# A cross-attention kernel in fp32: a new order for all operations, and two of the last half stores on ScalarE's queue

## The chip, the cores and the metric

The kernel runs on one core of one Trainium2 chip. The metric is the time of one execution in device microseconds (us). Before the change the median of three runs is 582.59 us. One execution was also profiled: every instruction with its engine, its start and its duration.

## The reference, cut to what matters

```python
query = hidden_states @ Wq                       # x: (2, 2048, 640)
keyt, valt = enc @ Wk, enc @ Wv                  # enc: the first 124 rows of ctx (2, 128, 384)
hs = _mha(query, keyt, valt)                     # 8 heads, softmax over 124 keys
ca_q1 = einsum('btc,th->bch', ca, Wq_ca)         # ca: the last 4 rows of ctx
ca_q1 = ca_q1[:, indices, :]                     # 384 rows stretched to 2048 by a fixed index
ca_hs1 = _mha(ca_q1, residual, residual)         # attention over the 2048 rows of x
ca_hs2 = _mha(ca_hs1 @ Wq, ca @ Wk_ca, ca @ Wv_ca)
out = (hs + ca_hs2) @ Wout + b_out + residual    # (2, 2048, 640), fp32
```

Because `ca_q1` has only 384 different rows, the second branch is computed once for 384 rows per batch and then gathered to 2048 by the index.

## The kernel before

**Units.** The 4096 rows of x are cut into 16 units of 256 rows, two tiles of 128 each. For each unit the kernel computes the text branch: scores of the queries against the 124 keys (`sc`), exponentials and row sums (`p`, `r`, in `softmax`, L2150), a multiply of `p` by the reciprocal sums (`share` in the same function, which POOL, VectorE or ScalarE may do; on ScalarE it is eight pieces, one for each head), a transpose to `eb`, and a store of `eb` to a buffer `kept` in HBM. Later the unit's probabilities come back in another layout in one load of 1 MB, `pT<-kept` (`probabilities`, L2214). There are two buffers for `pT`; a unit's load must wait until the unit that had the buffer has finished its last product `ph`.

**The output product.** `text_out_fast` (L2364) makes `ph` = values times `pT` in three products (`ph_m_0`, `ph_m_2`, `ph_m_4` for unit m; the last frees the `pT` buffer), copies them to `hs`, forms four sums s1 to s4 of halves of `hs` (`hs<-hs`, on VectorE or POOL), and multiplies them with `Wout` and sums of parts of `Wout` in four chains (`po_m_0` to `po_m_3`, a scheme after Strassen that saves one product in eight). After each step of a chain VectorE adds `po` into the unit's rows.

**The rows.** The rows hold x at first: `residual` (L2302) loads each tile of x into one of eight row buffers, four in the tile `x_more` and four in `last_rows`. When the additions to a tile are done, POOL adds the second branch by an indirect DMA (`add_second`, L2321, called "the gather" below), and a store sends the tile out (`stored`, L2479), which frees the row buffer for the next load. The last unit, 15, is different: its gathers come right after its loads, and it leaves in four half stores of 128x320, each as soon as its additions are done (`stored_half`, L2471).

**Other stages.** Around this run the loads and weights at the start, the queries of eight blocks of 512 rows, and the second branch (`s`, `ea`, `acc`, `y`, `away` and `landing` are names of it). Steps of all stages are interleaved on TensorE.

**What sets the order.** No loop order and no scheduler of the compiler: a recorder, `Desk` (L62), collects the operations of all stages as tasks. The table `TURNS` (L83) gives each operation of each task a number. `run` takes the operations in the order of these numbers; the number modulo 6 is the engine:

```python
ENGINES = ("PE", "ACT", "DVE", "POOL", "SP", "NONE")
op = min((op for q in self.queue.values() for op in q), key=turn)
engine = self.ENGINES[turn(op) % len(self.ENGINES)]
```

Each engine then executes its instructions strictly in that order. All loads and stores go out on SP's queue (`dma`, L443), so a load that must wait for a store to land, or a store that must wait for a gather, holds up every transfer behind it. The gathers go out on POOL, between POOL's own arithmetic. `Desk` also has a model of durations (`transfer`, L448, and the figures given to `dma`). The model only decides which free buffer an operation takes; the chip does not see it.

**How its lines read in the profile.** An instruction carries the line of the helper that issued it: L394 a product, L403 a product in four column groups of 32 (`by_columns`), L408 a transpose, L425 any instruction of VectorE, ScalarE or POOL, L445 a DMA on SP, L2323 a gather. So tiles, not lines, tell the steps apart. In the changed kernel these lines stand one further down.

Of the kernel before, what the change touches and what calls it, by code (L numbers as in the profile page):

```python
# [14 lines left out]
P = 128  # L15
# [50 lines left out]
class Desk:  # L66
# [376 lines left out]
    def dma(self, out, in_, us, issue=0.38, more=2.0):  # L443

        self.pin(self.nc.sync.dma_start(out, in_))  # L445
        self.transfer("SP", us, issue, more)
# [11 lines left out]
def kernel(  # L458
# [1343 lines left out]
    def y_rows(b, sb):  # L1802
# [3 lines left out]
        for u in range(2):  # L1806
# [11 lines left out]
            def away(t=op.value, u=u):  # L1818
                dma(kept[:, :, u, :], t.rearrange("p (a n) -> p a n", a=4), 0.8, 0.53)
# [743 lines left out]
```

## Time and profile before

| | us |
|---|---|
| median of 3 runs | 582.59 (581.97 to 584.22) |
| the profiled execution | 581.76 |
| its span, from the first to the last instruction | 579.8 |
| TensorE busy in it | 566.5 (98%) |
| VectorE busy | 390.7 (67%) |
| ScalarE busy | 290.9 (50%) |
| POOL busy | 160.3 (28%) |

PE is TensorE, DVE VectorE, ACT ScalarE, POOL GpSimd, SP the engine that issues the DMAs, and SPq its queue. A row of a timeline has the start in us, the duration, the engine, the line, the operation, out<-in and the shapes; x16 says that 16 like instructions were put together; square brackets hold the idle time of the engine ahead of the row and what ended it. A row of the waits has what the engine waited for, the sum in us, how often, and the longest. A row of the DMA issues has the size of one transfer in KB and the median us from issue to landing. The span is 1.96 us shorter than the profiled execution's time, which includes what lies around it.

### The profile page before, as it was taken

Reading aid. Unit: us, or ns where it says so; the run is one execution under the profiler, and the core shown is the slowest. Engines: PE = TensorE matmul, PEld = TensorE weight load, DVE = VectorE, ACT = ScalarE, POOL = GpSimd, SP = SyncE. Lnnn points to the kernel's source line nnn. Section 1 sums busy time; section 2 is a strip of 40 time slices with the busy share of each in tenths; the row PEclk is TensorE's granted clock in tenths of the full one; section 3 lists DMA queues with packets and bytes.
Section 4 is the critical chain, followed back from the end, with each engine's and each line's share of the span. In section 5 each row is a group of like instructions: output and inputs, shape, how many; then the busy total and the mean of one; then the engine's idle time right before and its main releaser. Section 6 shows DMA issues by size and latency. Waiting matters only on the chain.

```text
span 579.8 us, 18971 instructions
## 1 busy us (share of the span) xinstructions
PE 566.5 (98%) x8115; PEld 308.3 (53%) x8115; DVE 390.7 (67%) x663; ACT 290.9 (50%) x813; POOL 160.3 (28%) x213
## 2 busy tenths in 40 slices
PE   8999999999999999999999999999999999999996
PEld 8885334555555455565554554554554445455442
DVE  3356999999999656557999989996333225433352
ACT  1222264467665699899847762445554663101000
POOL 9102023411310127012025042423404032054171
PEclk9999999999999999999999999999999999999999
DMA  8998486756848796445464987978178457598987
GB/s 238 210 226 137 143 178 177 144 158 140 226 148 154 217 229 167 160 152 179 139 217 152 335 232 263 240 254 247 37 227 219 140 125 250 158 250 270 259 150 226
DMA packets 145213, 112.69 MB, mean 194 GB/s; under 512 B 82405, under 2 KB 116581, under 8 KB 145130
## 3 DMA queue, kind: packets, MB, share of 16 engines
q1 hardware_dynamic: 139498, 100.80, 60.1%
q0 software_dynamic: 5632, 10.69, 10.8%
q8 instruction: 64, 1.05, 0.8%
q14 instruction: 19, 0.16, 0.1%
HBM read 71.23 MB, written 40.22 MB: 192 GB/s over the span
## 4 chain that ended last, share of the span: by engine, by line
PE 75%; DMA 7%; DVE 7%; SPq 4%; ACT 2%; issue 2%; POOL 2%; DVEq 0%; ACTq 0%; POOLq 0%
PE po L403 23%; PE pq L403 19%; PE acc L394 7%; PE sc L394 6%; PE ph L394 6%; PE s L394 6%; PE pq L394 3%; SPq L445 3%; DVE mx L425 2%; DMA last_rows<-in_x_dram 2%; PE pyz L394 2%; DMA last_rows<-o,query 2%; DVE xt L425 1%; DMA xi<-in_x_dram 1%; ACT ea L425 1%
## 5 line engine op out<-in xcount | busy, mean ns | idle before, releaser
L425 DVE TENSOR_REDUCE mx<-s 128x4 f32<-128x2048 f32 x48 | 109.1, 2273 | 2.4 <-PE s L394 2.0
L425 ACT ACTIVATE p<-sc,m 128x124 f32<-128x124 f32 x256 | 90.4, 379 | 40.0 <-DVE m L425 40.0
L425 ACT ACTIVATE ea<-s 128x2048 f32<-128x2048 f32 x48 | 90.6, 1888 | 32.6 <-PE s L394 32.6
L425 POOL TENSOR_TENSOR p<-p,r 128x992 f32<-128x992 f32 x20 | 38.9, 1943 | 169.7 <-DVE r L425 148.8
L403 PE MATMUL po<-wout_sums,hs 128*32 128x320 f32 x1024 | 78.7, 433 | 1.4 <-POOL hs L425 1.4
L403 PE MATMUL po<-wout_sb,hs 128*32 128x320 f32 x928 | 72.1, 434 | 1.0 <-POOL hs L425 0.9
L403 PE MATMUL pq<-xt,wq_sb 128*32 128x256 f32 (+1 forms) x928 | 66.3, 418 | 0.0
L425 DVE TENSOR_TENSOR last_rows<-last_rows,po 128x320 f32<-128x320 f32 x64 | 30.3, 482 | 46.9 <-PE po L403 46.7
L425 ACT ACTIVATION_READ_ACCUMULATOR p<-sc,m 128x1 f32 x256 | 56.4, 220 | 0.0
L425 DVE TENSOR_TENSOR x_more<-x_more,po 128x320 f32<-128x320 f32 x64 | 30.5, 482 | 37.6 <-PE po L403 37.3
L394 PE MATMUL acc<-ea,y_sb 128*32 128x384 f32 (+2 forms) x768 | 50.4, 383 | 0.1
L403 PEld LDWEIGHTS po<-wout_sums,hs 128*32 128x32 f32 x1024 | 31.9, 110 | 35.0 <-POOL hs L425 2.7
L394 PE MATMUL ph<-pT,vpad 128*32 128x256 f32 x768 | 48.0, 380 | 1.0 <-DMA pT<-kept 1.0
L425 DVE TENSOR_REDUCE m<-sc 128x4 f32<-128x496 f32 x64 | 40.8, 663 | 11.6 <-PE sc L394 11.2
L425 POOL TENSOR_TENSOR hs<-hs 128x256 f32<-128x256 f32 x29 | 27.2, 1029 | 71.1 <-ACT hs L425 31.2
L403 PEld LDWEIGHTS po<-wout_sb,hs 128*32 128x32 f32 x928 | 29.0, 110 | 32.1 <-POOL hs L425 1.5
L425 DVE STREAM_TRANSPOSE eb<-p 128x1024 f32<-128x1024 f32 x32 | 39.5, 1236 | 5.6 <-POOL ca L425 2.4
L403 PEld LDWEIGHTS pq<-xt,wq_sb 128*32 128x32 f32 x928 | 28.1, 110 | 28.4 <-issue 12.7
L425 ACT COPY hs<-ph 128x512 f32<-128x512 f32 (+1 forms) x24 | 13.6, 573 | 54.2 <-PE ph L394 54.1
L2323 POOL DMA_INDIRECT x_more<-o,query x16 | 25.5, 1593 | 53.0 <-DVE x_more L425 45.5
L394 PEld LDWEIGHTS sc<-kmain,q 64*128 64x128 f32 x512 | 31.4, 187 | 14.5 <-issue 8.3
L394 PE MATMUL sc<-kmain,q 64*128 64x124 f32 x512 | 37.6, 284 | 0.2 <-ACT q L425 0.2
(219 smaller groups left out, 835.1 us busy)
## 6 DMA issues: line engine op xcount, KB each, us to landing
kept<-eb SPq DMA_DIRECT2D x32, 512.0 KB, 4.6
pT<-kept SPq DMA_DIRECT2D x16, 1024.0 KB, 7.6
landing<-away SPq DMA_DIRECT2D x15, 512.0 KB, 4.8
xi<-in_x_dram SPq DMA_DIRECT2D x56, 128.0 KB, 4.3
x_more<-in_x_dram SPq DMA_DIRECT2D x16, 320.0 KB, 5.2
last_rows<-in_x_dram SPq DMA_DIRECT2D x16, 320.0 KB, 4.0
out_dram<-x_more SPq DMA_DIRECT2D x15, 320.0 KB, 4.7
out_dram<-last_rows SPq DMA_DIRECT2D x15, 320.0 KB, 4.1
```

The costliest lines, as they stand in the source:

```text
L394: self.pin(self.nc.tensor.matmul(out, lhsT, rhs, **kw))
L403: self.pin(self.nc.tensor.matmul(out[j : j + 32], lhsT[:, j : j + 32], rhs, **kw))
L425: self.pin(getattr(engine, what)(*args, **kw))
L445: self.pin(self.nc.sync.dma_start(out, in_))
L2323: desk.pin(nc.gpsimd.indirect_dma_start(out=t, out_offset=None, in_=o2_of[b], in_offset=bass.IndirectOffsetOnAxis(ap=query[:, st : st + 1] ...
```

## The change

The diff replaces the whole table `TURNS`, so every engine has a new order and some operations a new engine. Of its rows only the last unit's half stores are shown, since the others tell a reader nothing: `.71` is the task of unit 15, `.71.3.9` to `.71.3.12` are its half stores, and the second number of each is the store's turn. In the new table two of them have remainder 1, which is ScalarE. The rest of the diff lets `dma` issue on ScalarE and gives other figures to the model of durations.

```diff
@@ -83,210 +83,211 @@
-        ".71.3.5": [11642], ".71.3.6": [12626], ".71.3.7": [13041], ".71.3.8": [13709], ".71.3.9": [13667, 13672],
-        ".71.3.10": [13643, 13648], ".71.3.11": [13697, 13702], ".71.3.12": [13721, 13726], ".71.3.13": [13392,
+        ".71.3.8": [13709], ".71.3.9": [13673, 13675], ".71.3.10": [13637, 13642], ".71.3.11": [13697, 13699],
+        ".71.3.12": [13721, 13726], ".71.3.13": [13476, 13556, 13584, 13598, 13608, 13622, 13680, 13712],
...
-        self.flights = {"SP": [0.0] * self.SLOTS, "POOL": [0.0] * self.SLOTS}
+        self.flights = {e: [0.0] * self.SLOTS for e in ("SP", "POOL", "ACT")}
...
     def dma(self, out, in_, us, issue=0.38, more=2.0):
 
-        self.pin(self.nc.sync.dma_start(out, in_))
-        self.transfer("SP", us, issue, more)
+        self.pin((self.nc.scalar if self.engine == "ACT" else self.nc.sync).dma_start(out, in_))
+        self.transfer(self.engine, us, issue, more)
...
-            dma(kept_of[m][:, :, k], eb.rearrange("p j h a -> p j (h a)"), 1.48, 0.53)
+            dma(kept_of[m][:, :, k], eb.rearrange("p j h a -> p j (h a)"), 1.6, 0.55, 1.6)
...
-            "SP", lambda: dma(pT.rearrange("p i k h a -> p i (k h a)"), by_keys, 2.8, 0.38),
+            "SP", lambda: dma(pT.rearrange("p i k h a -> p i (k h a)"), by_keys, 2.85, 0.42, 2.6),
...
-                dma(t, x[b, st * P : (st + 1) * P, :], 0.75, 0.37)
+                dma(t, x[b, st * P : (st + 1) * P, :], 0.95, 0.37)
...
-        desk.transfer("POOL", 1.7, 1.57)
+        desk.transfer("POOL", 2.0, 1.57, 2.2)
...
-        yield Do("SP", lambda: dma(out[b, st * P : (st + 1) * P, cols], t[:, cols], 0.43, 0.37, 1.8))
+        to = out[b, st * P : (st + 1) * P, cols]
+        yield Do(("SP", "ACT"), lambda: dma(to, t[:, cols], 0.43, 0.45, 2.2))
```

Counted over the program: TensorE has the same 4522 matrix instructions with the same shapes. Of the 32 multiplies of `p`, POOL has 11 (20 before), VectorE 8 (3), ScalarE 13 (9). Of the 64 sums `hs<-hs`, POOL has 32 (29) and VectorE 32 (35). Four of the 128x512 copies of `ph` go from ScalarE to VectorE. SP has 358 transfers (360), ScalarE 2 (0).

Three places of the order matter for what follows. The first is SP's order while units 4 and 2 fetch their probabilities. Names are tiles with their unit, `kept_11` being the probabilities of unit 11, `pT_4` those of unit 4 on their way back, `x_more` rows of x; a number at the end only counts tiles. Before (a second load of `x_more`, two rows behind the first, is left out):

```order
L445 DMA pT_4_4208<-kept_4_2134 128x4x512
L445 DMA y_sb_109<-y_1_1_2809 32x4x256
L445 DMA y_sb_109<-y_1_3_3204 32x4x256
L445 DMA away_7_4104<-wq_sums_836 32x4x256
L445 DMA y_sb_109<-y_1_2_2547 32x4x256
L445 DMA away_7_4104<-x_sums_864 32x4x256
L445 DMA kept_11_4185<-eb_11_1_4289 512x1x256
L445 DMA y_sb_109<-y_1_3_3204 32x4x256
L445 DMA x_more_3129<-in_x_dram 128x640
L445 DMA away_7_4104<-x_sums_864 32x4x256
L445 DMA zb_1_2_1_4359<-z_1_2_2548 128x512
L445 DMA pT_2_4344<-kept_2_1635 128x4x512
```

and now:

```order
L446 DMA landing_823<-away_6_3089 128x1x1024
L446 DMA y_sb_109<-y_1_0_2165 32x4x256
L446 DMA x_more_3071<-in_x_dram 128x640
L446 DMA y_sb_109<-y_1_1_2824 32x4x256
L446 DMA kept_11_4137<-eb_11_1_4260 512x1x256
L446 DMA zb_1_2_1_4296<-z_1_2_2564 128x512
L446 DMA pT_4_4245<-kept_4_2133 128x4x512
L446 DMA pT_2_4275<-kept_2_1640 128x4x512
L446 DMA o2_0_3976<-o2_0_2_4238 128x640
```

Unit 4's load has moved behind the store of `kept_11`, and unit 2's follows it at once.

The second place is SP's order when units 3, 12 and 9 fetch theirs, with the stores of finished rows (`out_0_dram`) and the loads of x into the same row buffers. Before:

```order
L445 DMA pT_3_5700<-kept_3_1923 128x4x512
L445 DMA pT_12_5745<-kept_12_4403 128x4x512
L445 DMA out_0_dram<-last_rows_4391 128x640
L445 DMA out_0_dram<-x_more_3129 128x640
L445 DMA last_rows_4391<-in_x_dram 128x640
L445 DMA x_more_3129<-in_x_dram 128x640
```

and now:

```order
L446 DMA x_more_3071<-in_x_dram 128x640
L446 DMA pT_3_5704<-kept_3_1915 128x4x512
L446 DMA out_0_dram<-last_rows_4257 128x640
L446 DMA last_rows_4257<-in_x_dram 128x640
L446 DMA out_0_dram<-x_more_3071 128x640
L446 DMA x_more_3071<-in_x_dram 128x640
L446 DMA pT_12_6017<-kept_12_4427 128x4x512
L446 DMA pT_14_6168<-kept_14_4836 128x4x512
L446 DMA pT_9_5766<-kept_9_3627 128x4x512
```

Unit 12's load no longer follows unit 3's; two stores and two loads of rows stand between, and each load comes right behind a store instead of behind both.

The third place is the end of POOL's order: sums of halves of `hs`, and gathers into `last_rows` and `x_more`. Before (the fourth and fifth rows are the gathers of unit 15, the sixth is the sum s2 of unit 8):

```order
L2323 DMA last_rows<-o_1_6359,query 128x640 x3
L425 TENSOR_TENSOR hs_4127<-hs_4127 128x256
L425 TENSOR_TENSOR hs_4229<-hs_4229 128x256 x2
L2323 DMA last_rows<-o_1_6359,query 128x640
L2323 DMA x_more<-o_1_6359,query 128x640
L425 TENSOR_TENSOR hs_4229<-hs_4229 128x256
L2323 DMA x_more<-o_1_6359,query 128x640 x2
L2323 DMA last_rows<-o_1_6359,query 128x640
L2323 DMA x_more<-o_1_6359,query 128x640
L2323 DMA last_rows<-o_1_6359,query 128x640 x2
```

and now:

```order
L426 TENSOR_TENSOR hs_4155<-hs_4155 128x256
L2324 DMA last_rows<-o_1_6386,query 128x640
L426 TENSOR_TENSOR hs_4247<-hs_4247 128x256
L2324 DMA last_rows<-o_1_6386,query 128x640
L2324 DMA x_more<-o_1_6386,query 128x640 x3
L2324 DMA last_rows<-o_1_6386,query 128x640
L2324 DMA x_more<-o_1_6386,query 128x640
L2324 DMA last_rows<-o_1_6386,query 128x640 x2
L2324 DMA x_more<-o_1_6386,query 128x640
L2324 DMA last_rows<-o_1_6386,query 128x640
```

The sum of unit 8 is gone from POOL (it is VectorE's now), and behind the last sum only gathers follow. Earlier on POOL, not shown, the sums s2 and s4 of unit 2 stand one gather and one multiply of `p` further ahead than before.

More of the change, by code (lines that the diff above doesn't have):

```diff
@@ L1679, in part_away @@
             def part_away(i, k=k, z=z):
-                dma(away[k, :, i].rearrange("q (g n) -> q g n", g=4), z[:, i].bitcast(F32), 0.45, 0.45)
+                dma(away[k, :, i].rearrange("q (g n) -> q g n", g=4), z[:, i].bitcast(F32), 0.31, 0.45)
             op = yield Do("ACT", lambda: desk.a_copy(z[:, 0], pq[:, cols]), [at], rank=0)
@@ L1706, in rest_back @@
         yield Do(
-            "SP", lambda: dma(t.rearrange("p g n -> p (g n)"), by_rows, 1.45, 0.5), [op.at], marks=[("landed", m)],
+            "SP", lambda: dma(t.rearrange("p g n -> p (g n)"), by_rows, 2.0, 0.56), [op.at], marks=[("landed", m)],
             rank=0,
@@ L1818, in away @@
             def away(t=op.value, u=u):
-                dma(kept[:, :, u, :], t.rearrange("p (a n) -> p a n", a=4), 0.8, 0.53)
+                dma(kept[:, :, u, :], t.rearrange("p (a n) -> p a n", a=4), 0.85, 0.53)
             yield Do("SP", away, frees=[(yts, op.slots[0][0])], marks=[("y out", b, sb, u)], rank=0.5)
@@ L2081, in second @@
             yield Do(
-                "SP", lambda: dma(o2_of[b][ct * P : (ct + 1) * P, :], o2, 1.1, 0.37),
+                "SP", lambda: dma(o2_of[b][ct * P : (ct + 1) * P, :], o2, 1.2, 0.37),
                 [("o2 part", b, ct, 0), ("o2 part", b, ct, 1)], frees=[(eas, k)],
```

405 rows, old and new, of the table TURNS are left out of this document.

## The prediction, as it was put on record before the changed kernel ran

> **What bounds the kernel now.** I read the page's busy times first, then the table of waits of TensorE, then the gaps in the timelines of PE, POOL and SP.
>
> ```profile
> PE 566.5 (98%) x8115; PEld 308.3 (53%) x8115; DVE 390.7 (67%) x663; ACT 290.9 (50%) x813; POOL 160.3 (28%) x213
> core 0: 579.8 us, clock 0.998
> PE po L403 <- POOL hs L425: 2.3, 2, 1.4
> PE s L394 <- ACT ea L425: 1.2, 2, 1.0
> PE unread L394 <- DVE zeros L425: 1.1, 1, 1.1
> PE ph L394 <- DMA pT<-kept: 1.0, 1, 1.0
> PE s L394 <- DVE mx L425: 0.6, 1, 0.6
> PE pt_x L408 <- DVE first_rows L425: 0.5, 1, 0.5
> PE sc L394 <- ACT q L425: 0.2, 1, 0.2
> ```
>
> TensorE is busy for 566.5 of 579.8 us at the full clock. The other 13.3 us are these waits (6.9 together), the tail behind the last product (about 5.7, below), and 0.7 of small change. So no order of the same work can take more than some 12 us off, and an order that starves TensorE can lose any amount. The diff leaves TensorE's work alone: the same products, each shape equally often, in another order. What decides is which of the seven waits go, which new ones come, and what the tail does. These are the gaps that the new order can reach:
>
> ```profile
> 333.86 1.07 PE L394 MATMUL ph<-pT,vpad 128*32 128x256 f32 x16 [1.00 <-DMA pT<-kept]
> 349.39 2.90 PE L403 MATMUL po<-wout_sb,hs 128*32 128x320 f32 x40 [0.92 <-POOL hs L425]
> 555.08 1.28 PE L403 MATMUL po<-wout_sums,hs 128*32 128x320 f32 x16 [1.38 <-POOL hs L425]
> ```
>
> The number in brackets is the idle time ahead. The waits for `ea`, `mx`, `q`, `first_rows` and `zeros` belong to steps whose neighbours read the same in both orders; I leave them as they are (3.6 together, 0 in the sum).
>
> **The sums on POOL: −2.30.** POOL ahead of the second and the third gap:
>
> ```profile
> 342.89 1.35 POOL L425 TENSOR_TENSOR hs<-hs 128x256 f32<-128x256 f32 x1
> 344.41 1.57 POOL L2323 DMA_INDIRECT x_more<-o,query  x1 [0.17 <-issue]
> 345.42 2.43 POOL L425 TENSOR_TENSOR p<-p,r 128x992 f32<-128x992 f32 x1
> 347.22 2.12 POOL L425 TENSOR_TENSOR hs<-hs 128x256 f32<-128x256 f32 x2
> ...
> 550.87 1.55 POOL L2323 DMA_INDIRECT last_rows<-o,query  x1 [12.40 <-DMA last_rows<-in_x_dram]
> 552.73 1.55 POOL L2323 DMA_INDIRECT x_more<-o,query  x1 [0.31 <-issue]
> 553.70 1.33 POOL L425 TENSOR_TENSOR hs<-hs 128x256 f32<-128x256 f32 x1
> ```
>
> At 347 the two sums of unit 2 stand behind a gather and a 2.43 us multiply of `p`; they end at 349.34 and the product starts at 349.39. In the new order both stand ahead of that gather, and the multiply is ScalarE's: at least 1.57 + 2.43 = 4.0 us less ahead of a product that was 0.92 late, so this wait goes whole. At 553 the sum of unit 8 stands behind the two gathers of unit 15, which themselves waited 12.40 us for unit 15's rows. In the new order unit 8's sums are all VectorE's, and POOL keeps only gathers behind that point: 1.38 goes. Together 0.92 + 1.38 = 2.30.
>
> The sum goes where 128x256 sums cost less, and the multiply goes to ScalarE as eight pieces:
>
> ```profile
> L425 DVE TENSOR_TENSOR hs<-hs 128x256 f32<-128x256 f32 x35 | 14.8, 432 | 12.7 <-ACT hs L425 7.6 <-POOL hs L425 4.9
> L425 ACT ACTIVATE p<-p,r 128x124 f32<-128x124 f32 x72 | 21.8, 389 | 4.3 <-DVE r L425 4.3
> 540.00:560.00 20.00, 18.62 (x292) 9.03 (x288) 9.09 (x22) 1.17 (x2) 7.92 (x6) 1.00 0.81 204
> ```
>
> Over the program 9 multiplies leave POOL, 5 go to VectorE and 4 (32 pieces, 32 × 0.389 = 12.4 us on the page's rate) to ScalarE; POOL takes 3 more `hs` sums net, and four copies of `ph` go from ScalarE to VectorE. VectorE is busy 9.09 of 20 us around the last sum (columns: length, then busy time and count of PE, PEld, DVE, ACT, POOL, then clock and DMA share), and ScalarE half of the span, so I cost these at nothing. Cover gone, one piece of 0.389 or one sum of 0.432 on the path would be the price.
>
> **Units 4 and 2 load their probabilities side by side: −1.00 + 0.60.**
>
> ```profile
> 314.50 0.57 SPq L445 DMA_DIRECT2D pT<-kept  x1
> 320.01 0.54 SPq L445 DMA_DIRECT2D kept<-eb  x1
> 325.82 0.43 SPq L445 DMA_DIRECT2D pT<-kept  x1
> ...
> 325.85 1.05 PE L394 MATMUL ph<-pT,vpad 128*32 128x256 f32 x16
> ...
> pT<-kept SPq DMA_DIRECT2D x16, 1024.0 KB, 7.6
> ```
>
> Unit 4's load left at 314.50 for a product at 325.85; unit 2's left at 325.82 for one that stood ready at 332.86 and started at 333.86. In the new order both leave one behind the other, behind the store of unit 11's probabilities (the row at 320.01). For unit 2 that is a lead of some 12 us against 7.6 to land: its wait of 1.00 goes. For unit 4 the lead shrinks. If nothing else moved, the load would leave at about 321.0 and have 4.9 us: 2.7 us late. But PE has two steps ahead of the product that stood behind it, a chain step (1.26 in the row at 572.87 below) and a small one of scores (0.5, an estimate): 6.7 us. And of the 5.5 us of issues between 314.50 and 320.01 several no longer stand ahead of the store; with half of them gone it is 9.5 us. So it is 0.9 late or not at all. I take 0.60, with 0 to 2.7 for the range.
>
> **Unit 12's load behind two store-and-load pairs: +0.70.**
>
> ```profile
> 434.73 3.75 SPq L445 DMA_DIRECT2D pT<-kept  x2
> 448.32 0.35 SPq L445 DMA_DIRECT2D out_dram<-last_rows  x1
> 448.78 0.37 SPq L445 DMA_DIRECT2D out_dram<-x_more  x1
> 453.96 0.34 SPq L445 DMA_DIRECT2D last_rows<-in_x_dram  x1
> 454.63 0.34 SPq L445 DMA_DIRECT2D x_more<-in_x_dram  x1
> ...
> 467.48 1.05 PE L394 MATMUL ph<-pT,vpad 128*32 128x256 f32 x16
> ...
> SPq L445 <- DMA out_dram<-last_rows: 25.0, 9, 6.8
> SPq L445 <- DMA out_dram<-x_more: 19.0, 8, 9.6
> ```
>
> Before, unit 12's load is the second of the row at 434.73, 30 us ahead of its first product at 467.48. In the new order it takes the buffer that unit 3's product frees, and stands on SP behind a store, a load into the same rows, a second store and a second load. A load into rows waits until their store has landed: 448.32 to 453.96 is 5.64 us, 448.78 to 454.63 is 5.85. Before, the two stores went out side by side and waited together; in the new order one pair follows the other: 448.32 + 5.64 + 0.34 + 5.85 + 0.34 = 460.5 for unit 12's load, 468.1 with 7.6 to land, 0.6 late; I round up to 0.70, since the first store may leave a little later too. Bounds: 0, if one pair is 0.7 quicker; if one store keeps SP waiting as long as the 9.6 of the last row, 0.7 + 3.75 = 4.5.
>
> **Other new waits: +1.00.** All 16 units' steps change places, and the loads of units 5 and 15 stand nearer to their products. The old table left three waits of about a microsecond at places that a reordering reaches (3.30 in all); nothing in the trace tells how many a new one leaves beyond the two that I found. I put one, at the size of the pT wait, 1.00, with 0 and 3.30 as bounds.
>
> **The tail: −0.40.**
>
> ```profile
> 572.87 1.26 PE L403 MATMUL po<-wout_sb,hs 128*32 128x320 f32 x16
> 573.66 1.03 DVE L425 TENSOR_TENSOR x_more<-x_more,po 128x320 f32<-128x320 f32 x2 [1.13 <-PE po L403]
> 572.30 2.84 SPq L445 DMA_DIRECT2D out_dram<-last_rows  x3
> 575.25 1.05 SPq L445 DMA_DIRECT2D out_dram<-x_more  x2
> 574.00:576.00 2.00, 0.13 (x4) 0.00 (x0) 0.64 (x2) 0.00 (x0) 0.00 (x0) 1.00 0.78 290
> ```
>
> The last product ends at 574.13, the last addition at 574.69; SP is still issuing until 575.14, so the last half store goes out about 1.05 us later than its data allow (575.74 against 574.69), and the span ends at 579.8. With two half stores on ScalarE, idle here, that 1.05 is the most to be had. The least is 0: the DMA engines are 0.78 busy from 574 to 576, with stores that were issued before. How long an issue on ScalarE takes no row here shows; the rows on SP (0.34) and POOL (1.55) bound it. Nearer to the busy DMA: −0.40.
>
> The Trainium skill, page "DMA: Bandwidth & Descriptors", section "Issuing engines are not separate DMA queues", says that transfers started by different engines share the same 16 DMA engines, and that a second issuing engine saves only issue time. By it this term lies between 0 and the 1.05 above; read strictly, with the engines as the limit, it is 0, and the sum would give 581.5. No row here shows a ScalarE store.
>
> **The sum.** −2.30 − 1.00 + 0.60 + 0.70 + 1.00 − 0.40 = −1.40 on the profiled execution: 581.76 becomes 580.36 (span 579.8 becomes 578.4). The median of the three runs is 582.59, 0.83 above the profiled one; the same step from there gives 581.2.
>
> **Rivals.** *The waits go and nothing comes back* (A). For it: three places have a cause that the order removes, and the two priced losses are within a microsecond of none. Against: a table of this size left seven waits before. −3.30 − 1.05 = −4.35: 578.2.
>
> *SP blocks at the head of its queue* (B, slower). The place is unit 12's load. For it: the two rows of SP's waits, 25.0 and 19.0 us in 17 waits, up to 6.8 and 9.6; before, nothing urgent stood behind them, now a load with no slack does. Against: it takes a long wait in one of two given pairs. With both at their longest: (9.6 − 5.85) + (6.8 − 5.64) = 4.9 more, so −1.40 + 4.9 = +3.5: 586.1. It turns slower than before from 1.4 us more waiting on.
>
> *The waits only move* (C). Each wait of before has a successor elsewhere, and the ScalarE stores bring nothing because the DMA engines finish the same transfers in the same time: 0, 582.6. For it: the kernel stands at 98% TensorE in both orders; against it, the named causes do go.
>
> **How the numbers follow.** Forecast 0.52 (581.2, own range 579.6 to 583), A 0.20, B 0.18, C 0.10. What a measurement of this kernel can tell from no change is about 0.5%, 2.9 us: below 579.7 counts as faster, above 585.5 as slower. A lies below 579.7, and some of the forecast: 0.20 + 0.07 = 0.27 faster. B lies above 585.5 in most of its cases, and the forecast with 3.30 and 2.7 at their upper bounds comes near: 0.17 + 0.02 = 0.19 slower. The rest, 0.54, is within. The range 577.8 to 585.4 leaves out the best of A (0.06) and the worse half of B (0.12).
>
> **What would show it.** In the table of TensorE's waits, `po <- POOL hs` gone or under 0.3 us; `ph <- DMA pT<-kept` at 1 to 2 us, at units 4 and 12, and not at unit 2; POOL behind 550 us with gathers alone; the last half stores issued within 0.5 us of the last addition, and the end under 5.7 us behind the last product. The forecast is wrong if a wait of over 2 us appears at `ph` (B), if new waits of TensorE for additions into row buffers or for PSUM banks add up to over 3 us, or if PE's busy time itself moves by over 1 us, as no term here allows for that.

## The result, and the profile after

The changed kernel runs in 578.02 us (median of 20 runs, 576.45 to 580.68); the kernel before, on the same chips, in 581.56 (20 runs, 579.08 to 584.22). The ratio is 0.9942, with a 95% interval of 0.9927 to 0.9957: 3.4 us less (2.5 to 4.2). The profiled execution took 578.33 us, its span is 576.5, against 581.76 and 579.8 before.

The page's busy times, and then the table of TensorE's waits, to be held against those in the prediction:

```profile
PE 566.8 (98%) x8115; PEld 311.3 (54%) x8115; DVE 395.6 (69%) x666; ACT 297.4 (52%) x840; POOL 151.3 (26%) x211
```

```profile
PE po L404 <- DVE x_more L426: 1.5, 2, 1.1
PE s L395 <- ACT ea L426: 1.2, 2, 1.0
PE s L395 <- DVE mx L426: 1.2, 2, 0.8
PE unread L395 <- DVE zeros L426: 1.1, 1, 1.1
PE pt_x L409 <- DMA xz<-in_x_dram: 0.2, 1, 0.2
PE acc L395 <- ACT ea L426: 0.2, 1, 0.2
```

The work is the same (566.8 against 566.5 us). All three waits that the prediction wanted to see go are gone: `po` no longer waits for a sum on POOL, and `ph` never waits for a load of probabilities. New are two waits for an addition into `x_more` and 0.6 us more for `mx`; together 5.4 us in place of 6.9. The larger of the new waits ends this stretch of the chain that ended last (start, duration, engine, step):

```profile
514.22 6.45 DMA x_more<-o,query
520.68 5.37 DMA out_dram<-x_more
526.12 7.73 DMA x_more<-in_x_dram
534.48 13.15 PE po L404 x192
```

and it reads like this in TensorE's timeline:

```profile
534.48 1.28 PE L404 MATMUL po<-wout_sums,hs 128*32 128x320 f32 x16 [1.06 <-DVE x_more L426]
```

A gather, the store that waits for it, the load into the same rows that waits for the store, and the addition that waits for the load and keeps a bank of TensorE occupied: 20 us of transfers in a row. This is rival B's mechanism, at another place and for 1.06 us.

At the place that the prediction named for it, unit 12's load behind two stores and two loads, SP's timeline and its waits from 448 to 460 us read:

```profile
448.67 0.34 SPq L446 DMA_DIRECT2D out_dram<-last_rows  x1
450.90 0.33 SPq L446 DMA_DIRECT2D last_rows<-in_x_dram  x1
451.33 0.38 SPq L446 DMA_DIRECT2D out_dram<-x_more  x1
454.86 0.33 SPq L446 DMA_DIRECT2D x_more<-in_x_dram  x1
458.08 0.37 SPq L446 DMA_DIRECT2D pT<-kept  x1
SPq L446 <- PE ph L395: 2.8, 1, 2.8
```

Each load goes out 2.2 and 3.5 us behind its store, in place of the 5.64 and 5.85 that were put. Both pairs are through at 455.19, and the load leaves at 458.08, right behind unit 3's last product, which ends at 458.02 and frees the buffer.

The tail, in the timelines of PE, DVE, SP, ScalarE's queue and POOL, and then in windows (the last two columns are the DMA engines' share and GB/s):

```profile
571.56 1.27 PE L404 MATMUL po<-wout_sb,hs 128*32 128x320 f32 x16
572.36 1.03 DVE L426 TENSOR_TENSOR last_rows<-last_rows,po 128x320 f32<-128x320 f32 x2 [1.13 <-PE po L404]
571.53 2.21 SPq L446 DMA_DIRECT2D out_dram<-last_rows  x2
571.26 0.38 ACTq L446 DMA_DIRECT2D out_dram<-x_more  x1
572.88 0.34 ACTq L446 DMA_DIRECT2D out_dram<-last_rows  x1
565.43 1.55 POOL L2324 DMA_INDIRECT last_rows<-o,query  x1 [2.08 <-DVE last_rows L426]
```

```profile
573.00:574.00 1.00, 0.00 (x0) 0.00 (x0) 0.38 (x1) 0.00 (x0) 0.00 (x0) 1.00 0.75 293
574.00:575.00 1.00, 0.00 (x0) 0.00 (x0) 0.00 (x0) 0.00 (x0) 0.00 (x0) 1.00 0.67 242
```

The last product ends at 572.83, 1.30 us earlier than before, and the span ends 3.67 us behind it in place of 5.67. The last half store is issued at once behind the last addition (which ends at 573.39). So in this pair of profiles 1.3 us come from the stream and 2.0 from the tail. The prediction's bound for the tail was 1.05, which made the tail the first thing to test.

### The profile page after: what moved, and what is told of

The parts are those of the page before. It is cut to its first block, busy times and chain, and to the rows that moved or that the text cites. A ratio compares the mean times of both kernels' runs of the same rounds, so it can differ in the third digit from the quotient of the medians.

```text
span 576.5 us, 18994 instructions
## 1 busy us (share of the span) xinstructions
PE 566.8 (98%) x8115; PEld 311.3 (54%) x8115; DVE 395.6 (69%) x666; ACT 297.4 (52%) x840; POOL 151.3 (26%) x211
## 3 DMA queue, kind: packets, MB, share of 16 engines
q8 instruction: 64, 1.05, 0.7%
## 4 chain that ended last, share of the span: by engine, by line
PE 73%; DVE 13%; DMA 5%; ACT 4%; issue 3%; POOL 0%; SPq 0%; DVEq 0%; ACTq 0%
PE po L404 24%; PE pq L404 13%; PE acc L395 7%; PE ph L395 6%; PE s L395 6%; DVE mx L426 5%; PE sc L395 5%; PE pq L395 4%; PE pyz L395 2%; ACT ea L426 2%; ACT p L426 2%; DVE eb L426 2%; DMA x_more<-in_x_dram 1%; PE pv L395 1%; PE pk L395 1%
## 5 line engine op out<-in xcount | busy, mean ns | idle before, releaser
L426 DVE TENSOR_TENSOR last_rows<-last_rows,po 128x320 f32<-128x320 f32 x60 | 28.2, 481 | 49.3 <-PE po L404 48.8
L426 DVE TENSOR_TENSOR x_more<-x_more,po 128x320 f32<-128x320 f32 x68 | 32.4, 481 | 42.4 <-PE po L404 40.7
L426 POOL TENSOR_TENSOR p<-p,r 128x992 f32<-128x992 f32 x11 | 20.4, 1852 | 117.1 <-DVE r L426 117.1
L2324 POOL DMA_INDIRECT x_more<-o,query x17 | 26.7, 1568 | 80.6 <-DVE x_more L426 47.7
L426 POOL TENSOR_TENSOR hs<-hs 128x256 f32<-128x256 f32 x32 | 25.7, 833 | 50.7 <-ACT hs L426 30.2
L426 POOL TENSOR_TENSOR x_sums<-xt,x_sums 128x512 f32<-128x512 f32 x10 | 13.7, 1365 | 84.8 <-DVE x_sums L426 84.5
```

Source lines behind the costliest of these rows:

```text
L426: self.pin(getattr(engine, what)(*args, **kw))
L2324: desk.pin(nc.gpsimd.indirect_dma_start(out=t, out_offset=None, in_=o2_of[b], in_offset=bass.IndirectOffsetOnAxis(ap=query[:, st : st + 1] ...
```

## The experiments

Twelve kernels were compared by ratios to the kernel before, timed beside them on the same chip; one execution of each was profiled. Where two variants are set against each other, it is by these ratios. An interval of 0.002 on either side is 1.2 us, so a single microsecond is near the limit of what a ratio can show. In the diffs the rows of `TURNS` are cut to the entries that change, and `...` marks other lines left out.

### Two half stores back on SP, and the reverse

The new order with the two stores on SP:

```diff
-        ".71.3.9": [13673, 13675]
+        ".71.3.9": [13673, 13678]
-        ".71.3.11": [13697, 13699]
+        ".71.3.11": [13697, 13702]
```

> The new order with the two half stores of unit 15 put back on SP's queue, at the same places between the other stores; nothing else differs from the changed kernel. In the profiles the tail (last product's end to the span's end) fell from 5.67 us to 3.67. Theory 1 (ScalarE's queue did it): without it the tail is back at 5 us or more and the time is 1.3 to 2 us above the changed kernel. Theory 2 (the order did it: unit 8's last gather lands 1.3 us ahead of the last product's end in place of 0.15, so fewer stores are left at the end): the tail stays under 4.4 us and the time is within 0.7 us of the changed kernel.

Measured: ratio 0.9925 (0.9899 to 0.9952, from six runs), tail 4.38 us. No loss is seen without ScalarE's queue; against the changed kernel's 0.9927 to 0.9957 the interval leaves room for one of up to 1.5 us.

The old order with the two stores on ScalarE:

```diff
-        self.pin(self.nc.sync.dma_start(out, in_))
+        self.pin((self.nc.scalar if self.engine == "ACT" else self.nc.sync).dma_start(out, in_))
...
-        yield Do("SP", lambda: dma(out[b, st * P : (st + 1) * P, cols], t[:, cols], 0.43, 0.37, 1.8))
+        to = out[b, st * P : (st + 1) * P, cols]; yield Do(("SP", "ACT"), lambda: dma(to, t[:, cols], 0.43, 0.37, 1.8))
...
-        ".71.3.9": [13667, 13672], ".71.3.11": [13697, 13702]
+        ".71.3.9": [13667, 13675], ".71.3.11": [13697, 13699]
```

> The old order with the same two half stores on ScalarE's queue; nothing else differs from the kernel before. Theory 1 (ScalarE's queue did it): the tail falls from 5.67 to about 4 us and the time by 1.3 to 2 us (ratio 0.997). Theory 2 (the order did it): the last half store still goes out on SP behind unit 8's full store, which waits for a gather that lands at 574; the tail stays above 4.9 us and the time within 0.7 us of the kernel before (ratio 0.999 to 1.000). My prediction's term lies between them: -0.4.

Measured: ratio 0.9985 (0.9968 to 1.0002), tail 5.87 us. ScalarE's rows at the end of its profile:

```profile
571.07 0.37 ACTq L445 DMA_DIRECT2D out_dram<-last_rows  x1
572.68 0.54 ACTq L445 DMA_DIRECT2D out_dram<-x_more  x1
```

Here and in the changed kernel an issue there takes 0.34 to 0.54 us, close to SP's. The ratio stands for a gain of 0.9 us, and its interval, from none to 1.9, does not part the two theories; the tail is as long as before, as theory 2 has it. Together the two runs speak for the order: by the ratios the gain is there without the queue. The tails are weaker evidence, since the changed kernel itself shows 3.67 us in one profile and 6.13 in another (below).

### The three sums alone

In the old order, unit 2's s2 and s4 ahead of a gather and a multiply, unit 8's s2 on VectorE:

```diff
-        ".58.3.6": [9123], ".58.3.7": [9147], ".64.3.6": [13287]
+        ".58.3.6": [9033], ".58.3.7": [9045], ".64.3.6": [13286]
```

> The old order with three sums moved: unit 2's s2 and s4 on POOL ahead of a gather and a multiply, unit 8's s2 from POOL to VectorE. Theory (the prediction's term of -2.30): both waits of TensorE for sums on POOL go, no other wait of over 0.3 us comes, the time falls by 2 to 2.6 us (ratio 0.996). Rival: the time freed at 349 us is spent at the next late thing (a gather or a scores bank), and the one at 555 us leaves the end where it was, since the last gathers and stores, not TensorE, set it; then less than 1 us (ratio over 0.998).

Measured: ratio 1.0013 (0.9996 to 1.0030). The prediction's largest term, −2.30, brings nothing by itself. The profile (an execution of 580.62 us, the shortest of the twelve) has no wait for a sum, but others in their place. Its table of waits, and then the timelines of TensorE, POOL, VectorE and SP:

```profile
PE s L394 <- DVE mx L425: 1.8, 3, 1.1
PE ph L394 <- DMA pT<-kept: 1.4, 2, 0.8
```

```profile
351.55 0.50 PE L394 MATMUL s<-zop,cop 32*128 32x512 f32 x4 [1.07 <-DVE mx L425]
363.33 1.07 PE L394 MATMUL ph<-pT,vpad 128*32 128x256 f32 x16 [0.85 <-DMA pT<-kept]
345.61 2.43 POOL L425 TENSOR_TENSOR p<-p,r 128x992 f32<-128x992 f32 x1
348.07 1.25 DVE L425 STREAM_TRANSPOSE eb<-p 128x1024 f32<-128x1024 f32 x1 [2.39 <-POOL p L425]
349.24 2.25 DVE L425 TENSOR_REDUCE mx<-s 128x4 f32<-128x2048 f32 x1
349.34 0.52 SPq L445 DMA_DIRECT2D kept<-eb  x1
351.64 1.10 SPq L445 DMA_DIRECT2D pT<-kept  x2
```

Read it downwards: the multiply of `p` on POOL ends at 348.04; the transpose to `eb` had waited 2.39 us for it; the maximum stands behind the transpose and ends at 351.49, and TensorE starts its next score product at 351.55. On SP the store of `eb` goes out, and behind it the loads of units 5 and 1; unit 1's landed at 363.20, and its product starts at 363.33. The kernel before has these rows at the same place (VectorE, TensorE, SP, TensorE):

```profile
347.89 1.25 DVE L425 STREAM_TRANSPOSE eb<-p 128x1024 f32<-128x1024 f32 x1 [1.53 <-POOL p L425]
349.06 2.26 DVE L425 TENSOR_REDUCE mx<-s 128x4 f32<-128x2048 f32 x1
352.22 0.50 PE L394 MATMUL s<-zop,cop 32*128 32x512 f32 x4
351.45 1.09 SPq L445 DMA_DIRECT2D pT<-kept  x2
362.83 1.07 PE L394 MATMUL ph<-pT,vpad 128*32 128x256 f32 x16
```

There the maximum ended at 351.32, 0.90 us ahead of its product, and unit 1's load landed at 362.40, 0.43 ahead of its own. A TensorE that comes 0.92 earlier just uses up the first and is 0.5 ahead of the second: the wait for the sums had covered them. But most of the 1.07 is the edit's own doing. With the sums ahead of it on POOL the multiply starts 0.2 us later than before, although TensorE is 0.7 us earlier there (its score product at 345.53 in place of 346.22), and the transpose waits 2.39 us for it in place of 1.53. A wait in the table is no price: the price is what is left when the next late thing is reached, and taking one operation ahead puts another back.

### The sums and that multiply

The three sums as above, and that multiply, of unit 13, on ScalarE (9037 has remainder 1):

```diff
-        ".69.2.2": [8774, 8792, 8833, 8845, 8863, 8953, 9032, 9081, 9134, 9172]
+        ".69.2.2": [8774, 8792, 8833, 8845, 8863, 8953, 9032, 9037, 9134, 9172]
```

> The old order with the three sums moved as in the earlier run, and one thing more: the multiply of p for unit 13's second tile goes from POOL to ScalarE, as in the new order. In the run with the sums alone that multiply ended at 348.04 and everything behind it was late: the transpose to eb (VectorE idle 2.39), the maximum behind the transpose (TensorE 1.07 at 351.55), and, behind eb's store on SP, unit 1's load (TensorE 0.85 at 363.33). Theory of the follower (the sums' wait only covered these): both waits go or fall under 0.3 us, unit 1's load leaves 2 us or more earlier, and the time falls against the kernel before by 1.5 to 2.5 us (ratio 0.996 to 0.9975). Rival: the end is set by the last transfers and a stream that is 2 us ahead only waits there: waits gone, ratio 0.999 or more. A second rival: the eight pieces on ScalarE delay the exponentials behind them by 1.7 us, and a new wait for a maximum or a bank takes the place of the old ones.

Measured: ratio 0.9995 (0.9977 to 1.0013). VectorE, SP and TensorE:

```profile
344.71 1.24 DVE L425 STREAM_TRANSPOSE eb<-p 128x1024 f32<-128x1024 f32 x1
345.87 2.25 DVE L425 TENSOR_REDUCE mx<-s 128x4 f32<-128x2048 f32 x1
349.47 1.09 SPq L445 DMA_DIRECT2D pT<-kept  x2
360.85 1.07 PE L394 MATMUL ph<-pT,vpad 128*32 128x256 f32 x16 [0.65 <-DMA pT<-kept]
```

The transpose comes 3.4 us earlier than in the run before this one, and the wait for `mx` there is gone, as the follower theory has it. But on SP two other transfers stand ahead of the loads, which leave only 2.2 us earlier, and unit 1's product still waits. The profiled span is 577.4, yet the median of the twelve runs hardly moves. So the theory is right on the chain and wrong on the price: of its 1.5 to 2.5 us the interval allows 1.3 at most. What both profiles share with the kernel before is in the next section.

### Where in the program the gain lies: mixed orders

Up to a point near 484 us both tables have done the same 2000 operations, so that one can be continued with the other; near 240 us (1040 operations) the same is true but for one operation. In outline:

```python
turns = {**first_2000(old), **the_rest(new)}
```

> The changed kernel once more, unaltered, as the measure for the two mixed orders of this call and for the two variants of the new order before it. Every theory expects a ratio of 0.993 to 0.995 as before, and a profile with the waits of the first one.

> A mixed order: the first 2000 of the 2288 operations in the old order, up to a point near 484 us at which both orders have done the same operations, the rest in the new order, its two ScalarE stores among it. Prediction's theory: of the gain the old waits at 334 and 349 us stay, and the one at 555 us goes with part of the tail: -1.38 - 0.4, ratio 0.997. Theory of the end (what counts is how early the last gathers and stores go): the whole gain is in the last 90 us: ratio 0.993 to 0.995, tail under 4.5 us. Theory that the gain is spread over many small waits in the first 484 us: ratio 0.998 or more.

> The complement: the first 2000 operations in the new order, the rest in the old order, with all stores on SP. Prediction's theory: -1.92 for the waits at 334 and 349 us, +1.3 for the loads of units 4 and 12 or nothing: ratio 0.997 to 0.999. Theory of the end: the whole gain is gone: ratio 0.999 or more, tail over 5 us. Theory of the first 484 us: ratio 0.994 to 0.996.

> A mixed order with an earlier seam: the first 1040 operations (to about 240 us) in the old order, the rest in the new. Both profiles have nearly the same waits of TensorE there (2.6 us before, 1.9 after), so every theory of a gain behind 240 us expects the new order's time, ratio 0.993 to 0.995. If the gain comes from the first 240 us after all (loads and queries, which the prediction left aside), the ratio is 0.997 or more.

| | ratio | interval |
|---|---|---|
| new order again | 0.9951 | 0.9930 to 0.9972 |
| old to 484 us, then new | 0.9978 | 0.9956 to 1.0001 |
| new to 484 us, then old | 0.9972 | 0.9952 to 0.9992 |
| old to 240 us, then new | 0.9968 | 0.9947 to 0.9988 |

By these ratios the new order is worth 1.3 us after 484 us and 1.6 before, together the whole, 2.9 here; with intervals of some 1.2 us on either side the sum may be so close by luck. The medians, 579.84 and 578.84 us for the two halves against 577.92 for the whole new order, speak against "all at the end" and "all ahead", the second less clearly. Of the part ahead of 484 us some may lie ahead of 240 (0.9968 against 0.9951); the intervals don't decide it.

For the part ahead of 484 us the traces show one thing that is the same in the profiles with the old order there and different in those with the new. It is the time between the landing of a unit's probabilities and the start of their first product (six profiles of the old order and seven of the new; the last variant below is not among them):

| load of unit | old order, us | new order, us |
|---|---|---|
| 2 | 0.13 to 0.26 | 3.2 to 4.3 |
| 1 | 0.13 to 0.56 | 13.5 to 14.2 |
| 4 | 2.2 to 3.9 | 0.6 to 1.8 |
| 5 | 5.6 to 6.4 | 0.5 to 1.7 |
| 12 | 23.8 to 23.9 | 0.7 to 2.5 |

In the old order units 2 and 1 are always within 0.6 us of being late, with waits of 0.55 to 1.84 in those profiles that show one. Unit 2's product comes ahead of the sums at 349, so that its wait is none of theirs; at unit 1 only the two profiles with the sums taken ahead have a wait (0.85 and 0.65). Unit 1's load goes out as the second of two, and took 10.2 to 10.9 us to land, where the first took 7.3 to 8.0. In the new order unit 1's load leaves alone, at 341:

```profile
341.03 0.41 SPq L446 DMA_DIRECT2D pT<-kept  x1
```

The new order has its own tight load, unit 5's: in the last variant below, whose order is the new one here, it was 1.16 us late.

This is the likeliest reason why freeing the sums brought nothing in the old order and is kept in the new. That the two loads alone are worth the 1.6 us was not tried, and 76 of the first 2000 operations also change their engine, which no run here sets apart.

### The end: gathers and row loads

Two profiles of the changed kernel end at 576.5 and 576.6 although TensorE ends at 572.83 in the one and, without the wait at 534, at 570.47 in the other. The second one's last rows of PE and SP in the timeline, and its windows:

```profile
569.20 1.27 PE L404 MATMUL po<-wout_sb,hs 128*32 128x320 f32 x16
567.27 1.62 SPq L446 DMA_DIRECT2D out_dram<-x_more  x2
570.34 1.04 SPq L446 DMA_DIRECT2D out_dram<-last_rows  x2
```

```profile
565.00:570.00 5.00, 5.00 (x80) 2.56 (x76) 1.87 (x6) 0.00 (x0) 0.00 (x0) 1.00 1.02 286
570.00:575.00 5.00, 0.47 (x8) 0.00 (x0) 0.96 (x2) 0.00 (x0) 0.00 (x0) 1.00 0.70 263
```

The tail is 6.13 us here, and it is full of stores. So four more variants were made. The first swaps two loads of rows, to take the wait at 534 away:

```diff
-        ".66.1": [12838, 12856], ".67.1": [12802, 12820]
+        ".66.1": [12820, 12856], ".67.1": [12802, 12838]
```

> The new order with two loads of rows swapped: unit 10's first tile is loaded ahead of unit 11's second. The changed kernel has its longest new wait, 1.06 us at 534.48, where an addition of unit 10 waited for the load that landed at 533.85 and held a bank. Theory: the wait goes or falls under 0.4 us, span 0.6 to 1.1 us shorter than the changed kernel's 576.5. Rival: unit 10's second tile (landed at 535.07) or unit 11's second tile is late next and takes the same microsecond; time as the changed kernel.

Measured: ratio 0.9912 (0.9890 to 0.9935), the wait gone, TensorE's end at 571.14, the span 576.2. The stream is 1.7 us ahead of the first profile's and the end 0.3. It is the best ratio of all, but its interval overlaps that of the changed kernel, whose own second profile lacks the wait too; it isn't shown to be faster.

Then the last two gathers, those of unit 8, were left out, once in each order, so that unit 8's rows lack the second branch:

```diff
-        op = yield Do("POOL", lambda: add_second(t, b, st), [*both, ("o2", b), "query"])
+        if m != 8: op = yield Do("POOL", lambda: add_second(t, b, st), [*both, ("o2", b), "query"])
```

> The new order without the two gathers of unit 8, the last ones of the program; the rows of unit 8 lack the second branch. Two profiles of the new order end at 576.5 and 576.6 although TensorE ends at 572.83 in one and at 570.47 in the other, with the DMA engines at 0.95 to 1.05 from 560 to 570. Theory of the drain (the last transfers, not TensorE, set the end): with two fewer of them the tail stays at 3.7 us or less with TensorE ending near 570.5 to 571.5, the span falls to 574.2 to 575.5 and the time by 1 to 2.3 us against the new order (ratio 0.991 to 0.993). Theory of TensorE: the span follows its last product and the ratio stays near 0.995.

Measured: ratio 0.9945 (0.9927 to 0.9963), tail 4.42 us: as the new order with them (0.9942 and 0.9951). The theory of the drain is not borne out for the gathers of the new order. What keeps the tail long when TensorE is early are more likely the stores themselves, six of which are issued within 3.8 us at the end of the second profile; no run tests that.

> The old order without the two gathers of unit 8; the rows of unit 8 lack the second branch. Theory of the drain: in the old order too the last stores queue behind the last gather (landed 573.98, with 0.96 of the DMA engines busy from 570 to 575); without it the tail falls from 5.5 to 5.9 to about 4.5 us and the time by 1 to 1.5 us (ratio 0.9975). Theory of TensorE: the sum of unit 8 on POOL still stands behind unit 15's gathers, the tail is as before and the ratio 0.999 to 1.000.

Measured: ratio 0.9977 (0.9954 to 1.0000), tail 4.14 us. By the ratio the two gathers do cost in the old order, about 1.3 us, as much as the new order's end is worth (0.9978), though the interval reaches a ratio of 1. In the profile before, the last gather landed at 573.98, 0.15 us ahead of the last product's end, with unit 8's full store behind it and the last two half stores behind that on SP; in the first profile of the new order it landed at 571.51, 1.32 us ahead. But in the second profile of the new order it landed at 570.32, again only 0.15 ahead, and the tail was 6.13. So the lead of the gather does not by itself explain why the new order ends earlier.

Last, the new order with unit 8's gathers moved ahead of its additions:

```diff
-        ".64.1": [13198, 13210]
+        ".64.1": [13198, 13210, 13239, 13245]
...
-        if m < UNITS - 1:
+        if m not in (8, UNITS - 1):
...
-        op = yield Do("POOL", lambda: add_second(t, b, st), [*both, ("o2", b), "query"])
+        if m != 8: op = yield Do("POOL", lambda: add_second(t, b, st), [*both, ("o2", b), "query"])
```

> The new order with the same work, but unit 8's two gathers moved ahead of its additions, right behind the load of its rows, as unit 15's are: they go out at about 548 to 550 us, where the DMA engines are 0.6 to 0.8 busy, in place of 562 and 565. Theory of the drain: tail under 4 us, 1 to 2 us less than the new order (ratio 0.991 to 0.993). Rival: the additions of unit 8 now wait for the gathers (some 5 us to land) and hold banks of TensorE, 1 to 3 us of new waits at 553 to 558, so that nothing is won or it is slower (ratio 0.995 to 0.999).

Measured: ratio 0.9992 (0.9965 to 1.0020), some 2.5 us slower than the new order. The rival was right, and a little too mild; TensorE and VectorE (the lines stand two higher in this kernel, and this execution, 584.75 us, is one of its longer ones):

```profile
560.91 1.28 PE L402 MATMUL po<-wout_sums,hs 128*32 128x320 f32 x16 [2.49 <-DVE last_rows L424]
560.37 0.49 DVE L424 TENSOR_TENSOR last_rows<-last_rows,po 128x320 f32<-128x320 f32 x1 [4.63 <-DMA last_rows<-o,query]
```

The addition waits 4.63 us for the gather and holds a bank, for which TensorE waits 2.49.

## Why the prediction was right, and where it was off

It said 581.2 with a range of 577.8 to 585.4, and 1.4 us less; measured were 578.02 and 3.4 less. One microsecond of the distance is the base: 582.59 was a median of three runs, and over twenty it is 581.56. The measured time lies only 0.2 us inside the range, and that it lies inside is in part luck: the largest term, −2.30, is not seen when it is tested by itself, and what the runs show in its place, unit 1's load and the end of the kernel, was in no term or far too small. Step by step:

- **What bounds the kernel.** Right: the products cost the same, and only waits and the tail moved. TensorE's busy time did differ by up to 3.0 us between profiles of the same products (565.8 to 568.8), so the condition "if PE's busy time moves by over 1 us" was too narrow.
- **The sums on POOL, −2.30.** The waits went as described, but the term was not worth its rows: 1.0013 for the sums alone, 0.9995 (at most 1.3 us of gain) with the multiply. What failed is the step from a wait in the table to a gain in time. Behind 0.92 stood unit 1's load and, put back by the edit, the multiply and the maximum. What stood behind 1.38 was not set apart; the last gathers and stores come next there, and leaving out those gathers gave some 1.3 us.
- **Units 4 and 2, −1.00 and +0.60.** The wait of unit 2 went (3.2 us to spare), and unit 4's load was 0.61 early, at a lead of 9.2 us, inside the 6.7 to 9.5 that were worked out. The 0.60 did not come; the place was rightly found to be tight.
- **Unit 12, +0.70.** The load left at 458.08 and landed in 7.02, where 460.5 and 7.6 were put; 1.44 to spare. The place was right and what sets the load's start was wrong: not the two pairs, which were through at 455.19, but unit 3's last product, at 458.02, with SP waiting 2.8 us for it.
- **Other new waits, +1.00.** The prediction left 3.6 us of waits standing. The first profile has 5.4, net 1.8 more (1.5 for `x_more`, 0.6 for `mx`, less at the start); the second has 4.0, net 0.4. The 1.00 was a fair size, though the waits came at places that it did not name.
- **The tail, −0.40.** In size −2.0 in the one profile and +0.46 in the other. The bound of 1.05 looked at issue times alone, and left out how late the last gathers and stores land. For ScalarE's queue by itself −0.40 stands within both measurements. With the term at 0 the sum gives 581.6, not the 581.5 stated. The Trainium skill, page "DMA: Bandwidth & Descriptors", section "Issuing engines are not separate DMA queues", has it that a second issuing engine saves issue time only. The two runs fit that without proving it: no loss is seen at 0.9925, and the other has a gain of 0.9 us with an interval from none to 1.9.
- **What was missing.** That unit 1's load left 11 us earlier stood in the order and was in no term, since the trace showed no wait there. It had landed 0.43 us before its product; that was to be read as the next wait.

Of the rivals, A (the waits go and nothing comes back, −4.35) is nearest to the 3.4 measured, with a cause only partly its own. At B's place nothing came late; its mechanism came at 534 us and cost 1.06 in one of two profiles. C's time fell, though its idea, that a wait only moves, is what the run with the sums alone showed.

What stays open: how the 1.6 us ahead of 484 us divide among the loads of units 1 and 2 and the rest of the new order, what shortens the end, and whether the first 240 us have a part. And in the old order with sums and multiply moved, the one profiled span fell by 2.4 us but the median of twelve did not follow.

## What to carry to other kernels

A wait of TensorE is worth only the distance to the next late thing: before pricing it, list what would be ready next on the other engines and queues, with the slack of each, and count slacks under half a microsecond as waits. When an operation is taken ahead on an engine, look at what it pushes back. When the order of the work changes, look at the transfers that land just in time, since they are late in some executions and no wait shows in others. At the end of a program compare the last transfer that another transfer waits for with the last product, and don't take one profile for the length of the tail.

## What the runs showed of the hardware that was not expected

The sixteen parts of one store can land far apart: the full store that went out at 567.70 in the second profile of the changed kernel had its first part done at 571.12 and its last at 573.94, while the last half store of the first profile had all parts between 575.03 and 575.60. That is 2.8 us for a store of 128x640 and 0.6 for one of 128x320. A load of 1 MB took 5.0 to 13.8 us to land over all profiles, and the second of two issued one behind the other longer than the first: 2.6 to 3.4 us longer for units 5 and 1 in the old order, 1.7 to 2.2 for units 4 and 2 in the new.
